# A decoder layer on one Trainium2 core: four sums of the seven-product stage change engine or place, and the routers' due times change

## The chip, the core and the metric

The kernel runs on one core of a Trainium2 chip. The core has five engines that run their own instruction streams and wait for each other by semaphores: TensorE (PE, matmuls), VectorE (DVE), ScalarE (ACT), GpSimd (POOL) and SyncE (SP, which here only issues DMAs). The metric is the device time of one execution in microseconds; the median of the runs counts. A profile of one execution shows what each engine did and when. Times in this document are microseconds from the start of the profiled span unless something else is said.

## The reference

The layer has three residual parts over x, 4 batches of 512 tokens with 512 features, all in float32: attention (32 query heads, 8 key heads, rotary, causal), a product with a context matrix that is rounded in blocks of 128, and a mixture of experts with one shared expert.

```python
x = x + attn(layernorm(x), wq, wk, wv, wo)
x = x + xattn(layernorm(x), ctx_2048)        # both sides rounded to 8 bits in blocks of 128
x = x + moe(layernorm(x), Wg, W1, W3, W2, sw1, sw3, sw2)

def moe(xt, ...):                            # 2048 tokens, 8 experts, 256 places each
    probs = softmax(xt @ Wg); eidx = argmax(probs); gate = probs[eidx]
    pos = place of the token among those of its expert; keep = pos < 256
    oe = (silu(xd @ W1[e]) * (xd @ W3[e])) @ W2[e]      # xd: the tokens sorted by expert
    shared = (silu(xt @ sw1) * (xt @ sw3)) @ sw2
    return oe[place] * gate * keep + shared
```

## The kernel before

**The attention loop.** A loop written out at build time goes over 80 pieces of attention, each of two half steps, n = 0 to 159, 40 half steps (SPB) for a batch. In each half step TensorE does scores (L939), turns the exponentials (L989) and multiplies with v (L1020); VectorE takes minima and ACT exponentials between them. These steps alone would leave TensorE waiting, so other work is put between them.

**The planner.** That other work is a list of jobs (L742 to L818), each a Python generator with a due half step, a cost in ns of TensorE time, a rank (`want`, or the due time where there is none; less 4 for the kinds in CHAIN) and the jobs that must be over before it. `Fill.upto` (L862) issues pieces of jobs in order of rank until its account of TensorE time reaches a goal. `share(n)` (L1066) sets how many ns a half step is to be filled with: it goes through the jobs in order of rank, adds up what is left of each in `ahead`, and for every q, k, v or o job takes `ahead` over the half steps that remain until it is wanted; the largest of these, kept between an even share (3522 to 3842 ns for batches 0 to 2) and 5284, is the quota.

```python
            ahead += job.left * (n < (B - 1) * SPB or job.key[0] not in CHAIN)
            if job.want > n + 20:
                break
            if job.key[0] in "qkvo":
                most = max(most, ahead / max(job.want - n, 1))
```

Some pieces ask for room on VectorE (`yield "dve", lag, us`) and some also for a moment in which GpSimd is idle by the planner's account (`"quiet"`; the helper `gpsimd(us, ...)` at L272 issues a GpSimd operation and adds `us` to that account). All of GpSimd's two-input operations are recorded at that helper's line, L273. A lag is counted in half steps of 7250 ns.

For each batch b the jobs that follow attention are: `o` (the output projection, four of them), `s` (sums of the second layernorm), `c` (the context matrix, rounded), `t` (four groups of 128 tokens: rounding, product with the context, sum into `acc`) and `w`, the **router**. The router (L617) writes the rows of `acc` to x2 in device memory by SP, makes the third layernorm, turns it and writes it to h3d by ACT's queue (L642), computes the logits (L655), counts the places by matmuls (L688, L689) and then scatters the rows to the experts' places xd by four indirect DMAs on GpSimd's queue (L719). It starts when all four `t` of its batch, and `cs` of the next batch, are over.

**After the loop** (from 1085 us) the shared expert is made in units (L1338 on): `shared_up(b, c)` for blocks c of 128 hidden columns, then two `shared_down(b, j)` for each batch. Between the matmuls of a unit, `between` (L1346) issues what is left of batch 3's jobs and of router 2, until nothing is left. A unit counts as one more half step, n = 161 and on. Batch 0 is made by plain matmuls (`up`, L1177). While its blocks run, `weight_sums(c)` (L1246) makes sums of the weights in place on GpSimd.

**The seven products.** For batches 1 to 3 and five of the blocks, `up7` (L1266) computes a 2 by 2 block product with seven products instead of eight. It needs sums of the token blocks, `token_sums(b)` (L1255), t1 to t4, in one buffer xSs for all batches, and the sums of the weights. Each product is four matmuls on 256 columns, gathered in a bank of PSUM: six of them go through the four banks with the tag "sp", product 3 has the single bank with the tag "av". In the version before, product 0 is copied by ACT (p1, L1283), products 1 and 2 are added by VectorE into u2 and u3 (L1284, L1285), product 3 is copied by ACT (p5, L1288) and added to u2 and u3 by two GpSimd sums (in the profile's rows u<-u,p and c<-u,p at L273), products 4, 5 and 6 are added by VectorE (L1291, L1295, L1297), and GpSimd makes the product of the two halves' results (gT<-gT,c).

`token_sums(1)` is called at the end of `shared_down(0, 0)`, `token_sums(b + 1)` at the end of `shared_down(b, 0)` (L1334). `shared_down` adds its two banks into xt on VectorE (L1329).

**The experts** follow (from 1314 us to 1560 us): rows of xd are loaded by SP (L1379), turned on TensorE (`turn_rows`, L257), and each expert's weights are loaded one expert ahead.

Of the kernel before, what the change touches and what calls it, by code (L numbers as in the profile page):

```python
# [23 lines left out]
def decoder_layer(  # L24
# [247 lines left out]
    def gpsimd(us, *args):  # L272
        nc.gpsimd.tensor_tensor(*args)  # L273
        work.gpsimd = max(work.gpsimd, work.at) + 1000 * us
# [469 lines left out]
    def add(due, cost, key, gen, *after, want=None):  # L744

        jobs.append(Job(due, cost, key, gen, after, want))

    MM4 = 4 * 860
    for b in range(B):
        z = b * SPB  # L750
        before = [(("acc", b - 2), 0.7)] if b > 1 else []
        add(z + 5, 0, ("x", b), load(load_x, b), *before)
        if b:
            add(z - 18, 0, ("wv", b), load(load_v, b), (("q", b - 1, 11), 0.5))
            add(z - 24, 0, ("hx", b), load(load_h, b), *([(("zero",), 0.7)] if b == 1 else []))
            add(z - 22, 0, ("hs", b), job_hs(b), (("hx", b), 1))
            add(z - 16, 1760, ("h", b), job_h(b), (("hs", b), 1.5), (("q", b - 1, 4 * NG - 1), 0))
        for j in range(TB):
            if b or j:
                add(  # L760
                    z - 16, MM4, ("v", b, j), job_v(b, j), (("h", b), 0.2), (("wv", b), 1.5),
                    want=z - 4 + 0.8 * j,
                )
        for a in range(NG):
            za = z + 10 * a
            if za:
                if a == 0:
                    before = ("q", b - 1, 4 * NG - 1)
                else:
                    before = ("q", b, 4 * a - 5) if a > 1 else ("v", b, TB - 1)  # L770
                n = b * NG + a
                add(
                    za - 20, 0, ("wk", b, a), load(load_k, b, a),
                    *([(("k", *divmod(n - 2, NG)), 0.5)] if n > 2 else []),
                )
                add(za - 20, 0, ("wq", b, a), load(load_q, b, a), (before, 0.5))
                add(
                    za - 10, MM4, ("k", b, a), job_k(b, a),
                    (("h", b), 0.2), (("wk", b, a), 1.5),
                    want=za - 4.5,  # L780
                )
            for r, due in enumerate((-9.5, -8.5, -7, -5)):

                want = 2 * r - 3.7 if a < NG - 1 or b == B - 1 else 0.8 * r + 1.1
                if za or r > 2:
                    add(
                        za + due, MM4, ("q", b, 4 * a + r), job_q(b, 4 * a + r),
                        (("h", b), 0.2), (("wq", b, a), 1.5), want=za + want,
                    )
            n = b * NG + a  # L790
            before = [(("o", *divmod(n - 1, NG)), 0.7)] if n else []
            if b == B - 1 and a > 1:
                before = [(("o", b, 1), 0.7)] if a == 3 else []
            add(za + 5, 0, ("wo", b, a), load(load_o, b, a), *before)
            add(za + 7, 110, ("r", b, a), job_r(b, a), want=za - 20)
            add(za + 8, 0, ("m", b, a), job_m(b, a), (("r", b, a), 1.5 if n < B * NG - 2 else 1), want=za - 20)
            add(za + 10, 0, ("n", b, a), job_n(b, a), (("m", b, a), 0), want=za - 20)
            add(
                za + 10, 4 * MM4, ("o", b, a), job_o(b, a),
                (("wo", b, a), 1.5), (("x", b), 1), (("n", b, a), 0.6),  # L800
                want=za + ((21, 21, 17, 16.5) if b < B - 1 else (22, 19.5, 18, 16.5))[a],
            )
        before = [(("t", b - 1, j), 0) for j in range(TB)] if b else []
        add(z + 6, 220, ("cs", b), job_cs(b), *([(("w", b - 2), 0.7)] if b > 1 else []))
        add(z + (22 if b else 12), 4 * 220, ("c", b), job_c(b), (("cs", b), 0.2), *before)
        ze = z + SPB + (5 if b < B - 1 else 0)
        add(ze, 0, ("s", b), job_s(b), (("o", b, NG - 1), 1))
        for j in range(TB):
            add(
                ze + 2 + (0, 3, 3, 2)[B - 1 - b] * j, 8 * 220, ("t", b, j), job_t(b, j),  # L810
                (("s", b), 0), (("c", b), 1), *([(("t", b, j - 2), 0)] if j > 1 else []),
            )
        add(ze + 5, 4 * 440 + 4000, ("w", b), job_w(b), *[(("t", b, j), 1) for j in range(TB)], *([(("cs", b + 1), 0)] if b < B - 1 else []))
    add(8, 0, ("zero",), job_zero())
    jobs.sort(key=lambda x: x.rank())
    for key in [("h", 0)]:
# [429 lines left out]
    def weight_sums(c):  # L1246

        a11, a12, a21, a22 = blocks(c)
        s2, s3, s4 = (wS[:, i, :, c * P : (c + 1) * P] for i in range(3))
        gpsimd(0.66, s3, a11, a21, ALU.subtract)  # L1250
        gpsimd(0.66, a21, a21, a22, ALU.add)
        gpsimd(0.66, s2, a21, a11, ALU.subtract)
        gpsimd(0.66, s4, a12, s2, ALU.subtract)

    def token_sums(b):  # L1255

        x = h3x[b]
        b11, b12, b21, b22 = (x[:, k : k + 2, t : t + T2] for k in (0, 2) for t in (0, T2))
        t1, t2, t3, t4 = (xSs[:, i] for i in range(4))
        gpsimd(1.27, t1, b12, b11, ALU.subtract)  # L1260
        gpsimd(1.27, t3, b22, b12, ALU.subtract)
        gpsimd(1.27, t2, b22, t1, ALU.subtract)
        gpsimd(1.27, t4, b21, t2, ALU.subtract)
        xS[b] = t1, t2, t3, t4, b11, b21, b22

    def up7(b, c, mid):  # L1266
        a11, a12, s1, a22 = blocks(c)
        s2, s3, s4 = (wS[:, i, :, c * P : (c + 1) * P] for i in range(3))
        t1, t2, t3, t4, b11, b21, b22 = xS[b]

        def product(i, w, x):
            ps = bank("av" if i == 3 else "sp", f"p7_{b}_{c}_{i}")[:, 0:T2]
            for k in range(2):
                nc.tensor.matmul(ps, w[:, k, :], x[:, k, :], start=k == 0, stop=k == 1)  # L1274
            return ps

        def part(tag, bufs=2):
            return gp.tile([P, T2], F32, tag=tag, bufs=bufs, name=f"{tag}_{b}_{c}")

        g = gTs[b][:, c, :]  # L1280
        p1, p5, u2, u3 = part("p1"), part("p5", 1), part("u2"), part("u3")
        c2 = gp.tile([P, T], F32, tag="c2", bufs=2, name=f"c2_{b}_{c}")
        nc.scalar.copy(p1, product(0, a11, b11))  # L1283
        nc.vector.tensor_tensor(u2, product(1, s2, t2), p1, ALU.add)  # L1284
        nc.vector.tensor_tensor(u3, product(2, s3, t3), u2, ALU.add)  # L1285
        if mid:
            mid(2500, 1.3)
        nc.scalar.copy(p5, product(3, s1, t1))  # L1288
        gpsimd(0.66, u2, u2, p5, ALU.add)
        gpsimd(0.66, c2[:, T2:T], u3, p5, ALU.add)  # L1290
        nc.vector.tensor_tensor(g[:, 0:T2], product(4, a12, b21), p1, ALU.add)  # L1291
        nc.scalar.activation(g[:, 0:T2], g[:, 0:T2], AF.Silu)
        if mid:
            mid(1700)
        nc.vector.tensor_tensor(g[:, T2:T], product(5, s4, b22), u2, ALU.add)  # L1295
        nc.scalar.activation(g[:, T2:T], g[:, T2:T], AF.Silu)
        nc.vector.tensor_tensor(c2[:, 0:T2], product(6, a22, t4), u3, ALU.add)  # L1297
        gpsimd(1.27, g, g, c2, ALU.mult)
        if mid:
            mid(1700, 1.0)  # L1300

    def shared_up(b, c, mid=None):
        if b not in gTs:
            gTs[b] = gp.tile([P, NHC, T], F32, tag="gT", bufs=2, name=f"gT_{b}")
        if b and c < HF:
            up7(b, c, mid)
        else:
            up(se["w"][0], h3x[b], gTs[b], c, T, f"s{b}_{c}", mid)
        if not b and c < HF:
            weight_sums(c)  # L1310
        if c == (HF - 1 if b else HF):
            se["next"] = b + 2
            load_h3(b + 2)
# [10 lines left out]
    def shared_down(b, j, mid=None):  # L1324
        for i in range(b * TB + j, b * TB + j + 2):
            xtile(i)
        for k, py in enumerate(down(gTs[b], se["w"][1], j, f"ys_{b}_{j}", "sp", mid)):
            i = b * TB + j + k
            nc.vector.tensor_tensor(xts[i], py, xts[i], ALU.add)  # L1329
            if i in routed:  # L1330
                nc.sync.dma_start(out=outf[i * P : (i + 1) * P, :], in_=xts[i])
            elif i not in kept:
                nc.sync.dma_start(out=x2[i * P : (i + 1) * P, :], in_=xts[i])
        if j == 0 and b < B - 1:  # L1334
            token_sums(b + 1)

    kept = set()
# [205 lines left out]
```

## Time and profile before

| what | us |
|---|---|
| median of three runs (lowest, highest) | 1594.07 (1592.9, 1597.47) |
| the profiled execution | 1587.93 |
| its span, first to last instruction | 1586.2 |
| TensorE busy | 1545.7 |
| VectorE busy | 849.8 |
| ACT busy | 529.5 |
| POOL busy | 405.1 |

By stage, from the windows view (us; busy time of each engine):

| stage | length | PE | DVE | ACT | POOL |
|---|---|---|---|---|---|
| 1085.4 to 1170.5: batch 0 of the shared expert, rest of the jobs | 85.1 | 84.46 | 49.13 | 14.58 | 40.89 |
| 1170.5 to 1215.6: seven products of batch 1 and half its "down" | 45.1 | 42.40 | 27.51 | 8.84 | 27.96 |
| 1230 to 1266: seven products of batch 2, router 3 | 36.0 | 35.28 | 16.95 | 10.56 | 12.20 |
| 1279.9 to 1316: seven products of batch 3 | 36.1 | 32.97 | 11.37 | 9.44 | 16.31 |
| 1316 to 1586.2: experts and the end | 270.2 | 264.62 | 47.06 | 25.84 | 16.33 |

How to read it: the profile's time line gives the start of an instruction, its length, its engine and line, the operation, what it writes and reads by the program's names, how many were merged into the row, and in brackets how long the engine sat idle before it and what ended that. A group's row has the busy time and mean ns of one after the bar, then the idle time before such instructions. A row of the windows view has the window, its length, and the busy time and number of instructions of PE, PEld (weight loads), DVE, ACT and POOL, the granted TensorE clock, and the DMA share and GB/s. The granted clock is 1.00 in all but two short stretches near 631 and 925 and at the very end.

### The profile page before, as it was taken

The numbers are of one execution on the slowest core, as the hardware profiler recorded it, in microseconds if no ns is written. First come the engines' busy times: TensorE is split into PE (matmuls) and PEld (weight loads), VectorE is DVE, ScalarE is ACT, GpSimd is POOL, SyncE is SP. The second block draws the span as 40 slices with busy tenths as digits, with TensorE's granted clock in tenths as the row PEclk, the third lists the DMA queues.
The fourth block names the chain that finished last, engine by engine and source line by source line (L and its number), as shares of the span: only waits on it lengthen the run. The fifth ranks groups of instructions, "written<-read, shape, count | busy, mean of one in ns | idle before, by whom it ended". The sixth has DMA issues, their size and how long they took to land.

```text
span 1586.2 us, 20493 instructions
## 1 busy us (share of the span) xinstructions
PE 1545.7 (97%) x6839; PEld 888.4 (56%) x6844; DVE 849.8 (54%) x2459; ACT 529.5 (33%) x1586; POOL 405.1 (26%) x370
## 2 busy tenths in 40 slices
PE   9999999999999999999999999999999999999998
PEld 5555555555544554555555545555455867776773
DVE  4465843458756566787656575665665431111114
ACT  2344453434444433443444444552111321110100
POOL 2021310303343031334312133143365340000004
PEclk9999999999999999999999999999999999999999
DMA  4474431524325253432525342256150350654646
GB/s 140 130 229 134 100 101 47 140 92 102 101 61 151 75 133 101 127 91 69 147 80 144 117 100 61 60 159 187 40 186 27 103 190 19 222 196 139 224 148 225
DMA packets 118346, 194.31 MB, mean 123 GB/s; under 512 B 17120, under 2 KB 36576, under 8 KB 117728
## 3 DMA queue, kind: packets, MB, share of 16 engines
q10 hardware_dynamic: 65472, 100.94, 22.7%
q1 hardware_dynamic: 50208, 83.67, 17.3%
q0 software_dynamic: 2560, 8.39, 1.6%
q8 instruction: 54, 0.88, 0.2%
q14 instruction: 52, 0.43, 0.1%
HBM read 135.54 MB, written 28.05 MB: 103 GB/s over the span
## 4 chain that ended last, share of the span: by engine, by line
PE 84%; DVE 5%; DMA 5%; POOL 2%; ACT 2%; issue 2%; SPq 1%; ACTq 0%; POOLq 0%; DVEq 0%
PE py L408 13%; PE psq L308 12%; PE p_e L1184 10%; PE sc L939 8%; PE av L1020 8%; PE pt L989 7%; PE p L1274 5%; PE epy L1212 4%; PE psv L350 4%; PE ys L1212 3%; PE psk L308 3%; PE p_s L1184 2%; DMA rrb<-rrd 1%; ACT pm L972 1%; PE ptr_h L257 1%
## 5 line engine op out<-in xcount | busy, mean ns | idle before, releaser
L972 ACT ACTIVATE pm<-pm,mn 128x256 f32<-128x256 f32 (+3 forms) x512 | 281.0, 550 | 381.5 <-DVE mn L962 352.5
L962 DVE CUSTOM_DVE_ANT_0 pm<-sc,mask 128x256 f32<-128x256 f32 (+3 forms) x512 | 216.8, 485 | 83.9 <-PE sc L939 83.6
L408 PE MATMUL py<-wo,aT 128*128 128x512 f32 x512 | 238.1, 599 | 1.5 <-issue 0.9
L308 PE MATMUL psq<-hT,wq 128*128 128x512 f32 x512 | 237.6, 601 | 1.7 <-DVE y L604 1.6
L273 POOL TENSOR_TENSOR t1q<-t1q,tsq 128x512 f32<-128x512 f32 x64 | 82.9, 1296 | 395.4 <-DMA tsq<-t2q 193.9
L939 PE MATMUL sc<-kT,t1q 64*128 64x384 f32 (+3 forms) x1024 | 169.2, 450 | 10.8 <-DVE pT L1006 3.5
L1006 DVE COPY pT<-pt 128x128 f32<-128x128 f32 (+3 forms) x256 | 114.0, 484 | 113.6 <-PE pt L989 106.0
L989 PEld LDWEIGHTS pt<-ident,pm 128*128 128x128 f32 x1280 | 145.0, 142 | 39.7 <-issue 28.7
L989 PE MATMUL pt<-ident,pm 128*128 128x128 f32 x1280 | 156.2, 275 | 4.1 <-DVE mn L962 4.0
L1184 PE MATMUL p_e<-h3x,slot_e 128*128 128x256 f32 x704 | 155.1, 380 | 0.0
L1020 PE MATMUL av<-pT,v 128*64 128x512 f32 (+3 forms) x1024 | 152.3, 439 | 1.2 <-ACT pT L1000 1.2
L308 PEld LDWEIGHTS psq<-hT,wq 128*128 128x128 f32 x512 | 92.3, 191 | 102.2 <-issue 97.7
L1000 ACT COPY pT<-pt 128x128 f32<-128x128 f32 (+3 forms) x256 | 96.9, 431 | 155.6 <-PE pt L989 123.6
L408 PEld LDWEIGHTS py<-wo,aT 128*128 128x128 f32 x512 | 92.1, 190 | 96.3 <-issue 88.6
L1184 PEld LDWEIGHTS p_e<-h3x,slot_e 128*128 128x128 f32 x704 | 132.6, 190 | 22.8 <-issue 5.3
L939 PEld LDWEIGHTS sc<-kT,t1q 64*128 64x128 f32 x1024 | 85.4, 186 | 94.3 <-issue 61.2
L1020 PEld LDWEIGHTS av<-pT,v 128*64 128x64 f32 x1024 | 68.3, 136 | 107.7 <-issue 95.6
L273 POOL TENSOR_TENSOR acc<-acc,y 128x512 f32<-128x512 f32 x64 | 81.0, 1270 | 136.1 <-DVE y L604 104.2
L972 ACT ACTIVATION_READ_ACCUMULATOR pm<-pm,mn 128x1 f32 x512 | 95.6, 187 | 0.0
L273 POOL TENSOR_TENSOR aT<-aT,rrb 128x512 f32<-128x512 f32 x64 | 82.0, 1311 | 18.6 <-DMA rrb<-rrd 9.7
L1196 DVE TENSOR_TENSOR wS<-p_e,wS 128x256 f32<-128x256 f32 x40 | 17.0, 424 | 119.3 <-PE p_e L1184 119.3
L1455 POOL DMA_INDIRECT slot_e<-oe,gidx x16 | 15.9, 996 | 243.7 <-DMA oe<-yo 239.1
(201 smaller groups left out, 1690.2 us busy)
## 6 DMA issues: line engine op xcount, KB each, us to landing
slot_e<-in_L_ffn_W_dram SPq DMA_DIRECT2D x14, 1280.0 KB, 12.3
wq<-in_L_attn_wq_dram ACTq DMA_DIRECT2D x16, 1024.0 KB, 6.4
tsq<-t2q SPq DMA_DIRECT2D x256, 64.0 KB, 2.3
wo<-in_L_attn_wo_dram ACTq DMA_DIRECT2D x16, 1024.0 KB, 5.6
rrb<-rrd ACTq DMA_DIRECT2D x32, 512.0 KB, 7.4
slot_e<-in_L_ffn_W_dram SPq DMA_DIRECT2D x7, 1408.0 KB, 6.7
kT<-t1k ACTq DMA_DIRECT2D x64, 128.0 KB, 2.9
wv<-in_L_attn_wv_dram ACTq DMA_DIRECT2D x4, 1024.0 KB, 6.1
```

The source lines that it names most:

```text
L273: nc.gpsimd.tensor_tensor(*args)
L308: nc.tensor.matmul(ps, w[:, k, c0 : c0 + P], hTs[b][:, k, :], start=(k == 0), stop=(k == KC - 1),)
L408: nc.tensor.matmul(py, aT[:, r, j * P : (j + 1) * P], wts["o", a][:, r, :], start=(r == 0), stop=(r == 3),)
L939: nc.tensor.matmul(scs[g][:, o : o + nk], qTs[b, p][g * HD : (g + 1) * HD, it * P : nk], kTs[b, p // 2][g * HD : (g + 1) * HD, 0:nk], star ...
L962: nc.vector.tensor_tensor_reduce(out=pm[:, o : o + nk], in0=scs[g][:, o : o + nk], in1=mask[:, T - nk : T], scale=-(HD**-0.5), scalar=3.0e ...
L972: nc.scalar.activation(pm[:, o : o + nk], pm[:, o : o + nk], AF.Exp, bias=mn, scale=-1.0, accum_out=rss[b, a][:, col : col + 1],)
L989: nc.tensor.transpose(pt[:, j * P : (j + 1) * P], pms[g][:, j * P : (j + 1) * P], ident)
L1000: nc.scalar.copy(pT[:, 0 : it + 1, it * P : nk], pt[:, o : o + nk].rearrange("p (j t) -> p j t", t=P),)
L1006: nc.vector.tensor_copy(pT[:, it + 1, 0:nk], pt[:, o : o + nk])
L1020: nc.tensor.matmul(av[g * HD : (g + 1) * HD, j * P : T], vs[b][:, j, v0 : v0 + HD], rhs, start=(j == 0), stop=(j == TB - 1),)
L1184: nc.tensor.matmul(pp[:, 0:cols], w13[:, k, o : o + P], xT[:, k, 0:cols], start=(k == 0), stop=(k == KC - 1),)
L1212: nc.tensor.matmul(py, gT[:, c, (t + i) * P : (t + i + 1) * P], w2[:, c, :], start=(c == 0), stop=False,)
```

## The change

There are four edits.

1. The due time of every router, and with it its rank, is later by four half steps.
2. `token_sums`: t3 comes first and stays on GpSimd; for the last batch t1, t2 and t4 are VectorE operations.
3. `up7`: product 3 is no longer copied; VectorE adds its bank into u2 and into the upper half of c2. The tile p5 goes, and the two GpSimd sums and their entries in the planner's account with it.
4. `token_sums(1)` is called in `shared_up(0, 2)`, after the weight sums of block 2, and no longer in `shared_down(0, 0)`.

```diff
-        add(ze + 5, 4 * 440 + 4000, ("w", b), job_w(b), *[(("t", b, j), 1) for j in range(TB)], ...
+        add(ze + 9, 4 * 440 + 4000, ("w", b), job_w(b), *[(("t", b, j), 1) for j in range(TB)], ...
...
-        gpsimd(1.27, t1, b12, b11, ALU.subtract)
         gpsimd(1.27, t3, b22, b12, ALU.subtract)
-        gpsimd(1.27, t2, b22, t1, ALU.subtract)
-        gpsimd(1.27, t4, b21, t2, ALU.subtract)
+        for out, x, y in (t1, b12, b11), (t2, b22, t1), (t4, b21, t2):
+            if b < B - 1:
+                gpsimd(1.27, out, x, y, ALU.subtract)
+            else:
+                nc.vector.tensor_tensor(out, x, y, ALU.subtract)
...
-        nc.scalar.copy(p5, product(3, s1, t1))
-        gpsimd(0.66, u2, u2, p5, ALU.add)
-        gpsimd(0.66, c2[:, T2:T], u3, p5, ALU.add)
+        p5 = product(3, s1, t1)
+        nc.vector.tensor_tensor(u2, p5, u2, ALU.add)
+        nc.vector.tensor_tensor(c2[:, T2:T], p5, u3, ALU.add)
...
         if not b and c < HF:
             weight_sums(c)
+            if c == 2:
+                token_sums(1)
...
-        if j == 0 and b < B - 1:
+        if j == 0 and 0 < b < B - 1:
             token_sums(b + 1)
```

More of the change, by code (lines that the diff above doesn't have):

```diff
@@ L812, in decoder_layer @@
             )
-        add(ze + 5, 4 * 440 + 4000, ("w", b), job_w(b), *[(("t", b, j), 1) for j in range(TB)], *([(("cs", b + 1), 0)] if b < B - 1 else []))
+        add(ze + 9, 4 * 440 + 4000, ("w", b), job_w(b), *[(("t", b, j), 1) for j in range(TB)], *([(("cs", b + 1), 0)] if b < B - 1 else []))
     add(8, 0, ("zero",), job_zero())
@@ L1275, in product, with part @@
             return ps
-        def part(tag, bufs=2):
-            return gp.tile([P, T2], F32, tag=tag, bufs=bufs, name=f"{tag}_{b}_{c}")
+        def part(tag):
+            return gp.tile([P, T2], F32, tag=tag, bufs=2, name=f"{tag}_{b}_{c}")
         g = gTs[b][:, c, :]
-        p1, p5, u2, u3 = part("p1"), part("p5", 1), part("u2"), part("u3")
+        p1, u2, u3 = part("p1"), part("u2"), part("u3")
         c2 = gp.tile([P, T], F32, tag="c2", bufs=2, name=f"c2_{b}_{c}")
```

## The prediction

> **What bounds the kernel.** I read the page first, then TensorE's waits, then the order of time around the longest of them.
>
> ```profile
> PE 1545.7 (97%) x6839; PEld 888.4 (56%) x6844; DVE 849.8 (54%) x2459; ACT 529.5 (33%) x1586; POOL 405.1 (26%) x370
> ...
> PE 84%; DVE 5%; DMA 5%; POOL 2%; ACT 2%; issue 2%; SPq 1%; ACTq 0%; POOLq 0%; DVEq 0%
> ```
>
> TensorE is busy for 1545.7 of 1586.2 us and is 84% of the chain that ended last. No matmul is added or removed, so all that the change can win or lose is TensorE's idle time: 40.5 us. Who ends it (line, waited for: us in total, times, longest):
>
> ```profile
> PE p L1274 <- DVE gT L1295: 3.8, 2, 3.1
> ...
> PE p L1274 <- DVE xt L1329: 2.6, 1, 2.6
> ```
>
> These 6.4 us lie in the seven-product stage that the edits touch; the windows before 1085 us hold some 26 us in about thirty small waits, and 1320 to 1560 us holds none. The 3.1 in order of time, GpSimd (POOL) first:
>
> ```profile
> 1279.33 1.01 POOL L719 DMA_INDIRECT xd<-h,r_dst_i  x1 [4.12 <-DVE r_flat L715]
> 1282.72 0.96 POOL L719 DMA_INDIRECT xd<-h,r_dst_i  x1 [2.38 <-DMA xd<-h,r_dst_i]
> 1285.69 0.96 POOL L719 DMA_INDIRECT xd<-h,r_dst_i  x1 [2.01 <-DMA xd<-h,r_dst_i]
> 1288.68 0.96 POOL L719 DMA_INDIRECT xd<-h,r_dst_i  x1 [2.02 <-DMA xd<-h,r_dst_i]
> 1289.66 0.73 POOL L273 TENSOR_TENSOR u<-u,p 128x256 f32<-128x256 f32 x1
> ```
>
> ```profile
> 1290.42 0.43 DVE L1295 TENSOR_TENSOR gT<-p,u 128x256 f32<-128x256 f32 x1 [5.64 <-POOL u L273]
> ```
>
> ```profile
> 1290.91 1.13 PE L1274 MATMUL p<-xS,wS 128*128 128x256 f32 x4 [3.13 <-DVE gT L1295]
> ```
>
> The last router's four scatters (L719) each wait for the one before to land, 10.3 us from first start to last end. The sum u of the first block of batch 3 stands behind them in POOL's queue, L1295 behind u, and TensorE runs out of the four "sp" banks.
>
> **Sums of p5 on VectorE.** Each of 15 blocks loses an ACT copy and two POOL sums and gains two VectorE sums that read the bank directly. Rows, by form:
>
> ```profile
> L1288 ACT COPY p<-p 128x256 f32<-128x256 f32 x15 | 5.6, 372 | 30.2 <-PE p L1274 30.2
> ```
>
> ```profile
> L273 POOL TENSOR_TENSOR c<-u,p 128x256 f32<-128x256 f32 x15 | 11.4, 763 | 0.0
> ```
>
> ```profile
> L1285 DVE TENSOR_TENSOR u<-p,u 128x256 f32<-128x256 f32 x15 | 6.4, 425 | 4.1 <-PE p L1274 3.6
> ```
>
> L1285 has the same form as the new sums: one input in PSUM, 256 columns. So ACT loses 5.6 us, POOL 11.4 + 10.9 = 22.3, VectorE gains 30 x 0.425 = 12.8. Per block VectorE carries seven such operations, 2.98 us, against seven products at 0.86 us (starts 1279.85, 1280.71 ...), 6.05 us on TensorE. In block (3,0) the product's bank is ready at 1283.58 (where the copy starts now), the sums end at 1284.43, L1291 starts 0.07 later than its 1284.36, and L1295 runs when product 5 is there, at about 1285.3. The 3.13 us go; next late is nothing in this block. POOL's product gT (1.27) still stands behind the scatters until 1291, but its reader is "down", and the first to need its buffer c2 is block (3,2), at about 1295.5. Behind the two new sums, which wait for product 3, VectorE holds L1291, L1295 and L1297, and TensorE's banks wait for those; in the trace product 3 always comes one product ahead of them. The one "av" bank is now held through two sums; it is wanted again 6 us later.
>
> In blocks with fillers a smaller piece: L453 and L241 took 0.83 (twice) and 0.58 us beside a POOL c sum, against 0.43 and 0.17 elsewhere, and TensorE's rows there are 2.29 and 2.08 long instead of 1.89, with a gap of 0.72 at 1243.67. Without the c sums about 0.4 + 0.2 + 0.4 = 1.0 us. Against it: 0.85 us more VectorE work ahead of the fillers; it lies under product 3 to 4. From both sides: 1.7 us gained, 1.5 lost (fillers of 2.8 us plus 0.85 outlast four banks). I take 1.0.
>
> The 2.57 us at 1172.55 I leave standing:
>
> ```profile
> 1169.25 3.31 DVE L251 TENSOR_SCALAR h<-acc,mvb,rsb 128x512 f32<-128x512 f32 x1
> ...
> 1174.38 1.28 DVE L1329 TENSOR_TENSOR xt<-ys,xt 128x512 f32<-128x512 f32 x2
> ```
>
> L251 takes 0.54 in its next row; here it lasted until POOL's acc sums ended at 1172.26, and L1329, which empties the banks, stood behind it. Neither POOL sum nor their order is touched. Bounds: 0 to 2.57 gained.
>
> **Token sums of batch 1**, four POOL sums of 1.27, move from 1152.44-1157.50 to behind block 2's weight sums, which end at 1127.9. POOL is idle 1128.6-1132.7 and 1135-1141; the weight sums of block 3 slip by 5 us and are needed from 1171 on. Their input h3x of batch 1 was asked for at 1085.5. Nothing behind 1157.5 waits for POOL's old place (0.69 us idle before its next sum, for VectorE's y). Cost 0.
>
> **Token sums of batch 3.** Three go to VectorE, behind L1329 (ends 1277.70), before L698. Nearest row: L454, the same form with both inputs in SBUF.
>
> ```profile
> L454 DVE TENSOR_TENSOR qv_x<-qv_x,qm_x x16: 691/692/1634, 378.5 to 1198.5; 128x512 f32<-128x512 f32 x16
> ```
>
> By its median: 3 x 0.69 = 2.08 us, t2 ready at 1279.1, product 1 wants it at 1280.71: hidden. The rule that speaks against the move is in the Trainium skill, "SBUF — State Buffer", Who interferes with whom: a VectorE instruction with two SBUF inputs and a GpSimd instruction reading SBUF exclude each other for the whole instruction. The row's maximum, 1634, shows one such loss of 0.94. If t1 and t2 each met a POOL sum of 1.27, t2 came at 1281.6, 0.9 late. POOL has one such sum then, t3, so I take the row, 0, and keep 0.9. If the router's end follows, it slips by 2.08; the scatters would land at 1293.5 instead of 1291.4, the first expert's rows at 1298.7 instead of 1296.6, wanted at 1307.4: hidden.
>
> **Routers put back.** The due times do not bind: router 0 starts at 506 us, in half step 72 by the count of attention blocks, router 1 in 110, router 2 in 156, router 3 in unit 177, against due 50, 90, 130, 165. All wait for their tokens' last job, so what a router issues (four writes of x2 on SP, four of h3d on ACT, four scatters on POOL, some sixty small VectorE operations) stays where it is in its queues, up to the order among jobs that are ready together. What moves is the rank, by 4: router b (46 + 40b) now comes behind o(b,3) (46.5 + 40b), so share() no longer counts its 5760 ns ahead of o(b,3). Stepping that arithmetic for the old order: half steps 38 to 44 have quotas of 4622, 4536, 4705, 4935, 5267, 5284, 5284 ns; with 5760 less ahead they become 3945, 3858, 4027, 4257, 4589, 5111, 5161, so 3.7 us of matmuls come later; likewise about 4 us in 79 to 84 and 2 us in 115 to 119. TensorE in those stretches and in the ones that follow:
>
> ```profile
> 282.00:327.00 45.00, 45.00 (x189) 22.93 (x188) 19.88 (x62) 17.22 (x57) 11.37 (x10) 1.00 0.47 118
> 327.00:375.00 48.00, 46.70 (x227) 25.10 (x226) 34.17 (x114) 20.13 (x66) 5.25 (x5) 1.00 0.46 131
> ```
>
> The first has no idle time, the second 1.3 us at a quota of 3842. Work moves from a stretch with cover to spare into one without. So 0, but from -4 to +7: every filler after half step 27 shifts a little, and the 26 us of small waits are dealt anew.
>
> **The end of router 3.** Stepping the planner: token sums of batch 1 and p5's sums leave its account of POOL, the quiet steps of t(3,2) and t(3,3) get in one unit earlier, and router 3's last step falls inside down(2,0) instead of after it. Then its scatters stand ahead of t3 in POOL's queue. Its counts matmul would be done near 1268.5 and the first scatter start near 1270.4; plus 10.3 and 1.27 gives t3 at 1282.0, product 2 wants it at 1282.44. Just hidden; each tick of two chunk pairs later costs 1.7 us, at most 5.3 (scatters from about 1276). I take 0.
>
> **Sum.** -3.1 - 1.0 = -4.1 us. The profiled execution took 1587.93 (span 1586.2 and 1.7 around it): 1583.8. It lies 6.1 below the median of the runs, 1594.07; I carry the difference over: 1590.0.
>
> **Rivals.**
> 1. *Quota* (slower). The withheld 10 us leave the attention chain uncovered. It decides above 4.1 us of new idle time. With two thirds lost, +7: 1597. For: the 3842 stretches have idle time. Against: those after them then have more cover. 0.18.
> 2. *t3 behind the scatters.* With 4 us of wait the gain is taken back: 1594. For: my stepping puts them in that order. Against: 0.4 us in hand. 0.15.
> 3. *More goes than I count.* L251 meets no POOL sum (-2.6) and the new deal saves 1.5 us: 1586. For: L251 started 0.53 before POOL's sum at 1169.78, so a small shift parts them. Against: nothing in their order changes. 0.20.
> 4. Forecast, -4.1 with about 2 to each side. 0.47.
>
> What can be told from no change is 0.3%, 4.8 us. Faster than 1589.3: all of 3, two fifths of 4: 0.38. Slower than 1598.9: a third of 1 and the worst of 2, with the tail of both: 0.14. Same: 0.48. The range takes in both ends of the loop's deal less their tails: 1582 to 1598.
>
> **What would show it.** No wait of p on L1295 near the scatters; POOL's u and c rows gone; VectorE sums at 0.42. A wait of p for POOL xS shows rival 2; idle time in half steps 38 to 44, 79 to 84 or 115 to 119 shows rival 1. The forecast is wrong if waits before 1085 us change by over 3 us.

## The result, and the profile after

| | before | after |
|---|---|---|
| median of the timed runs, us | 1595.25 | 1577.3 |
| ratio (95% interval) | | 0.989 (0.9868 to 0.9912) |
| the profiled execution, us | 1587.93 | 1577.95 |
| its span | 1586.2 | 1576.2 |
| TensorE busy, us | 1545.7 | 1543.5 |
| end of the attention loop in it | 1085.4 | 1074.1 |

Faster by 1.1%, below the range of the forecast (1582 to 1598). The page after, its engines and its chain:

```profile
PE 1543.5 (98%) x6844; PEld 887.5 (56%) x6844; DVE 858.7 (54%) x2492; ACT 523.5 (33%) x1571; POOL 380.4 (24%) x337
...
PE 74%; DMA 3%; DVE 3%; POOL 2%; issue 1%; ACT 1%; SPq 0%; ACTq 0%; POOLq 0%; DVEq 0%
```

TensorE's waits after (us in total, times, longest; L1274, L1295 and L1329 of before are now L1277, L1298 and L1334):

```profile
PE p L1277 <- DVE xt L1334: 2.6, 1, 2.6
...
PE p L1277 <- POOL xS L273: 1.4, 1, 1.4
...
PE p L1277 <- DVE gT L1298: 0.3, 1, 0.3
```

The wait of 3.1 us on VectorE's gT is gone as forecast, the 2.6 on xt stays as forecast, and a wait for POOL's xS is new: rival 2, at 1.4 us. All that is far from 18 us. The time is in the attention loop: from its end to the end of the span it is 500.8 us before and 502.1 after; the loop itself is 11.3 us shorter. (The 502.1 hold a stretch at half clock, 1.7 lost, and waits of 2.4 for GpSimd's aT, of which a second profile of the kernel after, e12, has 0.8.) Adding up TensorE's idle time over the loop gives 7.4 us less. A further 1.7 is one stretch at half clock less, and 2.2 more is spread thinly over matmul rows.

The largest single wait in the loop of before is in half steps 86 to 88. VectorE there:

```profile
624.61 0.16 DVE L238 TENSOR_SCALAR veb<-mvb 128x4 f32<-128x4 f32 x1
...
625.87 1.26 DVE L245 TENSOR_TENSOR r0b<-veb,rsb 128x4 f32<-128x4 f32 x1
...
628.14 0.69 DVE L317 TENSOR_TENSOR t2q<-psq,rt 128x512 f32<-128x512 f32 x1
...
629.61 0.45 DVE L251 TENSOR_SCALAR h<-acc,mvb,rsb 128x512 f32<-128x512 f32 x1
630.09 0.69 DVE L460 TENSOR_REDUCE am<-h 128x4 f32<-128x512 f32 x1
630.69 0.28 DVE L962 CUSTOM_DVE_ANT_0 pm<-sc,mask 128x128 f32<-128x128 f32 x1
```

and TensorE, before:

```profile
621.99 1.91 PE L989 MATMUL pt<-ident,pm 128*128 128x128 f32 x16
623.83 2.10 PE L939 MATMUL sc<-kT,t1q 64*128 64x128 f32 x12
625.86 2.37 PE L1020 MATMUL av<-pT,v 128*64 128x512 f32 x16
631.51 3.37 PE L989 MATMUL pt<-ident,pm 128*128 128x128 f32 x16 [3.27 <-DVE mn L962]
```

From 624.6 to 630.7 VectorE works off the root of batch 1's second layernorm (L238 on), three steps of attention itself (L317 among them) and the first token group (L251, L460). The minima (L962) that TensorE's transposes need stand behind them. One step of the root, L245, takes 1.26 where its neighbours take 0.16: it ends with a GpSimd sum that starts in the same moment, so 1.1 of the 3.27 us are that meeting.

```profile
625.86 1.26 POOL L273 TENSOR_TENSOR t1q<-t1q,tsq 128x512 f32<-128x512 f32 x1 [6.90 <-DVE rsb L247]
```

TensorE has nothing else to do: between transposes, scores and av stands no projection, which is the filler here (work of the planner's jobs). Its next transposes take 3.37 instead of 1.9, because half of the clock is withheld from 631.0 on. The same place after:

```profile
620.68 1.91 PE L989 MATMUL pt<-ident,pm 128*128 128x128 f32 x16
622.43 1.02 PE L308 MATMUL psq<-hT,wq 128*128 128x512 f32 x2
623.38 2.00 PE L939 MATMUL sc<-kT,t1q 64*128 64x128 f32 x12
625.31 2.37 PE L1020 MATMUL av<-pT,v 128*64 128x512 f32 x16
627.61 1.97 PE L989 MATMUL pt<-ident,pm 128*128 128x128 f32 x16
```

No wait stands between these rows. By the planner's account the root's step is now issued in half step 89 instead of 87, behind these minima.

**A second figure for each run.** Each run lists the mean granted clock of TensorE. Over 95 runs of the kernel before it lies between 0.988 and 0.998, and the time falls by 1.5 us for each 0.001 that it is higher; time times clock is 1584.1 with a scatter of only 1.3 from run to run. I call this product the time at full clock: a stretch at half clock counts half in it. It separates waits from clock. The kernel after has 1571.6 (8 runs), so 12.5 us of the gain are waits and matmul time, and the rest of about 4 is the clock, 0.9933 to 0.9958. With four to twenty runs a figure at full clock is good to some 0.3 to 0.8 us, no better.

### The profile page after: what moved, and what is told of

The parts are those of the page before. It is cut to its first block, busy times and chain, and to the rows that moved or that the text cites. A ratio compares the mean times of both kernels' runs of the same rounds, so it can differ in the third digit from the quotient of the medians.

```text
span 1576.2 us, 20462 instructions
## 1 busy us (share of the span) xinstructions
PE 1543.5 (98%) x6844; PEld 887.5 (56%) x6844; DVE 858.7 (54%) x2492; ACT 523.5 (33%) x1571; POOL 380.4 (24%) x337
## 4 chain that ended last, share of the span: by engine, by line
PE 74%; DMA 3%; DVE 3%; POOL 2%; issue 1%; ACT 1%; SPq 0%; ACTq 0%; POOLq 0%; DVEq 0%
PE py L408 12%; PE p_e L1184 10%; PE psq L308 9%; PE av L1020 7%; PE sc L939 7%; PE pt L989 6%; PE p L1277 6%; PE epy L1212 4%; PE psv L350 3%; PE p_s L1184 2%; PE ys L1212 2%; PE psk L308 2%; DMA tsq<-t2q 1%; POOL aT L273 1%; PE ptr_h L257 1%
## 5 line engine op out<-in xcount | busy, mean ns | idle before, releaser
L962 DVE CUSTOM_DVE_ANT_0 pm<-sc,mask 128x256 f32<-128x256 f32 (+3 forms) x512 | 216.6, 486 | 91.1 <-PE sc L939 91.1
L308 PE MATMUL psq<-hT,wq 128*128 128x512 f32 x512 | 236.5, 599 | 2.4 <-DVE y L604 2.3
L939 PE MATMUL sc<-kT,t1q 64*128 64x384 f32 (+3 forms) x1024 | 165.5, 448 | 6.7 <-ACT pT L1000 2.5
L308 PEld LDWEIGHTS psq<-hT,wq 128*128 128x128 f32 x512 | 91.9, 190 | 102.1 <-issue 96.4
```

The source lines that it names most:

```text
L308: nc.tensor.matmul(ps, w[:, k, c0 : c0 + P], hTs[b][:, k, :], start=(k == 0), stop=(k == KC - 1),)
L939: nc.tensor.matmul(scs[g][:, o : o + nk], qTs[b, p][g * HD : (g + 1) * HD, it * P : nk], kTs[b, p // 2][g * HD : (g + 1) * HD, 0:nk], star ...
L962: nc.vector.tensor_tensor_reduce(out=pm[:, o : o + nk], in0=scs[g][:, o : o + nk], in1=mask[:, T - nk : T], scale=-(HD**-0.5), scalar=3.0e ...
```

## The experiments

Two groups of theories. For the whole: is it edit 1 (quota) or edits 2 to 4 (sums)? For the quota: "smoothing" (the gain follows the work that is withheld) or "deal" (it comes from where a few VectorE pieces fall).

| run | what | median, us | ratio to before (95%) | at full clock |
|---|---|---|---|---|
| e1_due_only | edit 1 alone | 1581.25 | 0.9915 (0.9898 to 0.9932) | 1573.2 |
| e2_no_due | edits 2 to 4 alone | 1589.14 | 0.9967 (0.9953 to 0.998) | 1582.0 |
| e3_share_only | only share() sees it | 1581.3 | 0.9913 (0.9895 to 0.9931) | 1573.6 |
| e4_before_again | the kernel before | 1594.02 | 0.9996 (0.9982 to 1.001) | 1584.2 |
| e5_three_quarters | routers count 3/4 | 1590.9 | 0.9979 (0.9961 to 0.9997) | 1581.0 |
| e6_share_batch1 | share(), router 1 | 1588.9 | 0.9956 (0.994 to 0.9972) | 1580.7 |
| e7_share_batch2 | share(), router 2 | 1588.7 | 0.9966 (0.9955 to 0.9977) | 1580.6 |
| e9_p5_only | edit 3 alone | 1598.34 | 1.0018 (1.0007 to 1.0028) | 1585.3 |
| e10_t3_vector | after, t3 on VectorE | 1574.83 | 0.9878 (0.9857 to 0.9899) | 1571.0 |
| e11_three_waits | after, three moves | 1575.23 | 0.9875 (0.9842 to 0.9908) | 1569.9 |
| e12_after_again | the kernel after | 1578.83 | 0.9898 (0.9877 to 0.992) | 1571.9 |
| e13_two_waits | after, two moves | 1571.4 | 0.9856 (0.983 to 0.9883) | 1569.2 |

**Which edit.** e1 has the first diff in the kernel before, e2 its reverse in the kernel after; e4 is the kernel before.

```diff
-        add(ze + 5, 4 * 440 + 4000, ...
+        add(ze + 9, 4 * 440 + 4000, ...
```

> The kernel before with the routers' due time alone later by four half steps (edit 1); POOL sums, token sums and their places as before. Its order of work up to the end of the attention loop is that of the changed kernel. Theory A (the gain lies in the attention loop, where the smaller quotas deal TensorE's small waits anew): the loop ends about 11 us earlier than before (1074 instead of 1085 us), the stage after it is as before with its wait of 3.1 us on L1295, and the profiled span is about 1575 us; timed 16 to 18 us below before. Theory B (the gain comes from the POOL sums taken off in the seven products): span within 2 us of 1586, timed within 3 us of before.

> The changed kernel with the routers' due time put back to that of before (edits 2 to 4 alone). Its order up to the end of the loop is that of before. Theory A: the loop ends at 1085 us as before, and the stage after it is 1 to 2 us longer (the wait of 3.1 us on L1295 is gone, waits on POOL for aT and for t3 come): span 1586 to 1588 us, timed within 3 us of before. Theory B: span about 1577 us, timed 15 us or more below before.

> The kernel before, unchanged, for the spans and granted clocks of its timed runs. The profiled execution of before took 1587.93 us, its timed runs 1592.9 to 1597.5, while the changed kernel's profiled and timed runs agree. If short stretches of half clock after waits of 2.5 to 3.3 us come in some executions and not in others, the slower runs have the lower mean clock (each stretch of 3.4 us at half clock costs 1.7 us): 1595 us would go with a clock of about 0.993 against 0.997. If the clock is the same, the 7 us are idle time that comes from something else.

Edit 1 alone brings 10.9 us at full clock, edits 2 to 4 alone 2.1; together they would be 13.0, and 12.5 was measured. The gain of edit 1 was put to zero in the prediction. The sizes expected here were off as well: the median of e1 fell by 12.6 and not by 16 to 18, and e2 came out 4.8 below before and not within 3.

**Rank or quota.** e3 leaves every rank as it was and lets `share` alone count the routers later:

```diff
+        def later(x):
+            return x.rank() + 4 * (x.key[0] == "w")
-        for job in sorted(todo, key=lambda x: x.rank()):
+        for job in sorted(todo, key=later):
...
-            if job.want > n + 20:
+            if later(job) > n + 20:
```

> The kernel before, where only share() counts the routers four half steps later; due times and ranks of the jobs themselves stay. Theory A1 (quota): as e1, span about 1575 us. Theory A2 (the rank among jobs that are ready together): as before, span 1586 us.

1573.6 at full clock against 1573.2 in e1: the quota explains all of it within the noise.

**What in the quota.** e5 counts the routers at 3/4 in their old place. e6 and e7 let share() move one router only, otherwise as in e3 (e7 has 2 for the 1):

```diff
-            ahead += job.left * (...)
+            ahead += job.left * (0.75 if job.key[0] == "w" else 1) * (...)
...
+            return x.rank() + 4 * (x.key == ("w", 1))
```

> The kernel before; share() counts the routers at three quarters of their cost, in their old place. By the planner's account this brings its loop near the put-back one's at two places: the second layernorm's last step for batch 1 leaves half step 87 for 89, and the last group of tokens of batch 0 leaves half step 71 for 69; but it takes little off the quotas (half step 43: 5283 to 4394, half step 78: 5283 to 4438, half steps 79 to 84 unchanged or higher). Theory 'smoothing' (time falls with the work withheld): a quarter of the count, so about a quarter of the 12.6 us of the share-only kernel, near 1590.5. Theory 'deal' (what counts is between which minima and transposes a few pieces with VectorE work fall): most of the gain, the idle time of 3.3 us near 628 and those of 1.4 to 1.6 near 419, 447 and 484 gone, loop end near 1076 instead of 1085.4, median near 1583.

> The kernel before; share() counts the router of batch 1 alone four half steps later. Quotas fall in half steps 79 to 84 only (5141 to 4373, 5096 to 4168), about 4 of the 10 us withheld; the last output projection of batch 1 ends in half step 85 instead of 84, but the second layernorm's root and the first token group's piece still stand in half steps 87 and 88. Theory 'smoothing': four tenths of 12.6, near 1589. Theory 'deal': the 3.3 us near 628 stay, the median within 2 us of 1593.9.

> The kernel before; share() counts the router of batch 2 alone four half steps later. Quotas fall in half steps 115 to 119 (5283... of before is 4464 to 3880 there), order unchanged before 114. Theory 'smoothing': two tenths of 12.6, near 1591.4. Theory 'deal': the wait of 2.51 near 921 becomes 1.4 and its half-clock stretch of 3.41 us (1.7 lost) goes: 1.1 + 1.7 to 4, near 1590.5; nothing before half step 114 moves. The two theories are told apart here only by the place: idle time must change near 921 and nowhere else.

"Deal" missed twice. In e5 the pieces moved as it said, but only 3.1 us at full clock were gained: the waits near 419, 447 and 484 went and that at 628 fell to 1.19, but waits of 2.41 at 351.6, 2.67 at 587.0 and 2.40 at 861.1 came. In e6 the wait at 628 went although the root stayed ahead of the minima (only L251 and L460 moved behind them, to 629.61). TensorE and VectorE in e6:

```profile
619.70 1.91 PE L989 MATMUL pt<-ident,pm 128*128 128x128 f32 x16
621.45 4.46 PE L308 MATMUL psq<-hT,wq 128*128 128x512 f32 x10
625.84 2.00 PE L939 MATMUL sc<-kT,t1q 64*128 64x128 f32 x12
627.76 2.37 PE L1020 MATMUL av<-pT,v 128*64 128x512 f32 x16
```

```profile
626.91 0.16 DVE L247 SCALAR_TENSOR_TENSOR rsb<-r0b,rsb 128x4 f32<-128x4 f32 x1
627.01 0.29 DVE L962 CUSTOM_DVE_ANT_0 pm<-sc,mask 128x128 f32<-128x128 f32 x1
```

Ten projection matmuls (L308) stand where before has none: the lower quota of half steps 79 to 84 left them over, and they cover the root. "Smoothing" has the number of e5 (1590.5) and e6 (1589), but not of e7: the wait near 921 fell from 2.51 to 1.38, waits of 0.59 near 867 and 0.47 near 936 went, nothing before half step 114 moved, and yet 3.5 us at full clock were gained, as much as in e6. Its shares, four and two tenths, came from the prediction's 10 us. The quotas that share() gives when the kernels are built fall by 23.7 us in all for e3, by 18.6 for e5, 5.4 for e6 and 2.1 for e7, against gains of 10.5, 3.1, 3.4 and 3.5: the gain does not follow the work withheld.

So neither theory stands as stated; what the traces show is a number of single waits. The one at 628 needs two things at once, a VectorE piece ahead of what TensorE waits for (e8 below takes it away) and no filler to cover it (e6 supplies it). The old quota made the second: by the planner's account all filler that was ready was spent by half step 87, and 87 and 88 had none. At 484 it looks the same: before has no projection between 478 and 491, after has fourteen there, of which twelve are

```profile
485.62 5.31 PE L350 MATMUL psv<-wv,hT 128*128 128x512 f32 x12
```

At 447 and 921 projections stand right beside the wait, so the pair of conditions is shown for 628 alone. By e6 and e7 routers 1 and 2 bring 3.4 and 3.5; the first would have 3.6 by difference from e3, but was not run alone, and e6 removes the wait at 628 in another way (by filler) than the kernel after (the root later).

e8 moves the root, and with it the token group that follows it. A second hunk of its edit acts after the loop, so only its loop can be compared (one execution, 1598.42):

```diff
-        yield "quiet", 0.3, 2.0
+        yield "quiet", 2.0 if b == 1 else 0.3, 2.0
```

> The kernel before; of batch 1 the root of the second layernorm (some sixteen small VectorE operations, 3.5 us) is held for two half steps instead of 0.3, so that it falls into half step 89 and no longer ahead of half step 88's minima; and token sums that come before their rows first finish that batch's router, so the part after the loop is not comparable and only the loop is read. Theory 'deal': the idle time of 3.27 us near 628 (pt waits for mn) is gone, under 0.5, with quotas up to there as before; half step 88 ends 3 us earlier, 5 if the half-clock stretch goes with it. Theory 'smoothing': the idle time stays, since the quotas up to there are those of before.

```profile
626.18 2.37 PE L1020 MATMUL av<-pT,v 128*64 128x512 f32 x16
628.49 1.97 PE L989 MATMUL pt<-ident,pm 128*128 128x128 f32 x16
```

The transposes follow av at once, with the quota of before up to there: this wait has the named cause. (Later in the loop e8 met waits of 1.4 to 1.6 at 696, 724 and 762, like those that before has one batch earlier, at 419, 447 and 484: a gain at one place moves the next.)

**Edit 3 alone,** in the kernel before (one line of it):

```diff
-        gpsimd(0.66, u2, u2, p5, ALU.add)
+        nc.vector.tensor_tensor(u2, p5, u2, ALU.add)
```

> The kernel before with edit 3 alone (product 3 added by VectorE from its bank, no copy, no GpSimd sums). Theory 'as forecast' (each edit's cost stands alone): the 3.13 us on L1295 go and nothing comes: about 3 to 4 us below the kernel before, near 1591. Theory 'edits belong together': router 3's end comes one step earlier by the planner's account, its four scatters stand ahead of the last batch's token sums, which here are all on GpSimd in the order t1, t3, t2, t4; t2 comes 2.5 us after the place at which edits 2 to 4 together have t3 (1.37 us of wait for product 2), and product 1 wants it 0.86 earlier: 1.37 + 2.54 + 0.86 = 4.8 us of wait for POOL xS. Then the sum is -3.1 - 1 + 4.8 = +0.7, near 1595.5.

```profile
PE p L1274 <- POOL xS L273: 4.7, 1, 4.7
```

The wait is as worked out (4.8): the sums on VectorE alone make the kernel slower, by 1.2 us at full clock where 0.7 was worked out, since router 3's scatters then stand ahead of all four token sums. The rest of the median's 1598.3 is clock (0.9922 on average). Edits 2 and 4 together pay for edit 3; they were not run apart. In the kernel after, POOL and TensorE at that place:

```profile
1263.03 1.01 POOL L719 DMA_INDIRECT xd<-h,r_dst_i  x1 [1.37 <-DVE r_flat L715]
1266.05 0.96 POOL L719 DMA_INDIRECT xd<-h,r_dst_i  x1 [2.01 <-DMA xd<-h,r_dst_i]
1269.02 0.96 POOL L719 DMA_INDIRECT xd<-h,r_dst_i  x1 [2.01 <-DMA xd<-h,r_dst_i]
1272.60 0.96 POOL L719 DMA_INDIRECT xd<-h,r_dst_i  x1 [2.62 <-DMA xd<-h,r_dst_i]
1273.59 1.27 POOL L273 TENSOR_TENSOR xS<-h3x 128x512 f32<-128x512 f32 x1
```

```profile
1274.91 1.13 PE L1277 MATMUL p<-xS,wS 128*128 128x256 f32 x4 [1.36 <-POOL xS L273]
```

**Taking more waits away.** e10 adds t3 to the three sums on VectorE. e13 adds the second edit below, e11 all three; e12 is the kernel after.

```diff
-        gpsimd(1.27, t3, b22, b12, ALU.subtract)
-        for out, x, y in (t1, b12, b11), (t2, b22, t1), (t4, b21, t2):
+        for out, x, y in (t1, b12, b11), (t2, b22, t1), (t3, b22, b12), (t4, b21, t2):
...
-        yield "dve", 0, 1.3
+        yield "quiet" if b == B - 1 and j > 1 else "dve", 0, 1.3
...
-        yield "dve", 0.8 * pace(b), 1.6
+        yield "dve", 0.4 if b == 0 else 0.8 * pace(b), 1.6
```

> The changed kernel with t3 of the last batch on VectorE as well. The wait of 1.36 us of product 2 for POOL's xS behind the four scatters goes; VectorE has 0.69 more ahead of the scatters' indices, hidden. Theory 'rival 2 is what held the tail back': -1.4 of the changed kernel's time, near 1575.9, TensorE waits for nothing between 1265 and 1280 by more than 0.3. Other theory: another reason (banks, VectorE) is late right behind it, and the time stays at 1577.

> The changed kernel with three waits of TensorE above 1.3 us aimed at: t3 of the last batch on VectorE (1.36); the first pieces of the last two token groups of batch 3 only when GpSimd is idle by the planner's account (the 2.57 at 1163, L251 held by GpSimd's sums ahead of L1334); router 0's last VectorE operations with a lag of 0.4 instead of 0.8 half steps (the 2.43 at 584, where nine of its operations of 0.16 took 1.1 to 1.2 us each beside GpSimd's four aT products). If all three go: 6.4 us, and the half-clock stretches that followed two of them in the changed kernel's profile, 1.7 each in part of the runs: 1577.3 - 6.4 - 2 = near 1569. If the moved pieces meet another GpSimd operation instead, the waits come back at other places and the time stays within 3 us of the run with t3 alone.

> The changed kernel once more, for more runs beside the others: 1577.3 within 2 us. Its idle time by half step should repeat within 0.3 us of the first profile's at every wait above 1 us; half-clock stretches of 3.41 us, if there are any, should follow waits of TensorE above about 1.2 us and not fall at the same places in each profile.

> The changed kernel with two of the three moves of the run before: t3 of the last batch on VectorE, and the first pieces of the last two token groups of batch 3 only when GpSimd is idle by the planner's account; router 0's end as in the changed kernel. If the 2.57 us at 1163 are a VectorE operation held by GpSimd's sums ahead of L1334, they go here as well: idle time 1.36 + 2.57 = 3.9 less than the changed kernel, and the half-clock stretch behind 1163 with them. From the 1574.8 of t3 alone: -2.6 and up to 1 for the clock, near 1571.5; the wait of 2.4 to 2.8 near 585 stays. If the other move was what took the wait at 1163 away (by its shift of the loop), the wait comes back and the time is 1574.8.

e10: the 1.36 us are gone, and nothing over 0.3 came behind them. At full clock that is 0.6, with an uncertainty as large; the rest of its 2.5 to 4 us in the median is clock. e12: its median is within the 2 us, but the wait near 585 was 2.80 there against 2.43, more than the 0.3 allowed, and two of its half-clock stretches stand at the same waits as in the first profile of after. e13: the wait at 1163 is gone, 1571.4 where 1571.5 was expected. The row that had held it, L251, took 3.31 ahead of the banks' L1334 in the kernel after; in e13 it takes 0.54 behind them (L1333 and L1276 of e13 are L1334 and L1277 of after):

```profile
1156.91 1.29 DVE L1333 TENSOR_TENSOR xt<-ys,xt 128x512 f32<-128x512 f32 x2 [1.31 <-PE ys L1222]
...
1160.04 0.54 DVE L251 TENSOR_SCALAR h<-acc,mvb,rsb 128x512 f32<-128x512 f32 x1
```

TensorE then runs without a gap there:

```profile
1156.81 1.13 PE L1276 MATMUL p<-h3x,slot_s 128*128 128x256 f32 x4
1157.77 1.89 PE L1276 MATMUL p<-xS,wS 128*128 128x256 f32 x8
```

e13 is the best version: 1.4% below the kernel before (1.2 to 1.7), and some 6 us below the one after. e11 missed: its third move should have freed the wait of 2.4 to 2.8 near 585. In the kernel after, VectorE there:

```profile
579.86 1.11 DVE L704 TENSOR_TENSOR r_flat<-r_flat,r_cnt 128x4 f32<-128x4 f32 x1
581.01 1.19 DVE L708 TENSOR_TENSOR r_dst<-r_flat,spill 128x4 f32<-128x4 f32 x1
...
583.45 1.19 DVE L710 TENSOR_TENSOR r_dst<-r_dst,spill 128x4 f32<-128x4 f32 x1
...
585.42 0.69 DVE L317 TENSOR_TENSOR t2q<-psq,rt 128x512 f32<-128x512 f32 x1
```

```profile
579.69 4.93 POOL L273 TENSOR_TENSOR aT<-aT,rrb 128x512 f32<-128x512 f32 x4
```

```profile
586.81 2.83 PE L408 MATMUL py<-wo,aT 128*128 128x512 f32 x3 [2.43 <-issue]
```

Router 0's small operations take 0.16 each elsewhere. Beside the four GpSimd products, from 579.69 to 584.62, L704 to L710 take about as long as one product each, and L317, the first to read a bank, stands behind them all. (The profile names no engine for TensorE's 2.43; that it is a bank is inferred from L319, behind L317, which ends at 586.71.) Moving the small operations freed them, and a larger operation met the same products. VectorE, GpSimd and TensorE in e11:

```profile
581.52 7.04 DVE L456 TENSOR_TENSOR qq_c<-qv_c,qm_c 128x512 bf16<-128x512 f32 x1
```

```profile
581.88 4.91 POOL L273 TENSOR_TENSOR aT<-aT,rrb 128x512 f32<-128x512 f32 x4
586.76 1.25 POOL L273 TENSOR_TENSOR t1k<-t1k,tsk 128x512 f32<-128x512 f32 x1
```

```profile
588.62 0.40 PE L257 MATMUL ptr_c<-ident_b,qq_c 128*128 128x128 bf16 x4 [3.68 <-DVE qq_c L456]
```

The wait there grew to 3.68. An order that frees both wasn't tried.

## Why the prediction was wrong, and where it was right

By its steps:

- **Sums of p5 on VectorE, -3.1:** right. The wait is gone, and the new sums take what L1285 took, by the group's row after. (The scatters came earlier too, so no run tells whether the sums alone would have been enough.)

```profile
L1292 DVE TENSOR_TENSOR u<-p,u 128x256 f32<-128x256 f32 x15 | 6.4, 424 | 7.1 <-PE p L1277 7.1
```

- **Fillers, -1.0:** right. The gap of 0.72 at 1243.67 is 0.32 after, and the rows of 2.29 and 2.08 are 1.89. From the first of the seven products to the last there are 143.9 us in before and 141.4 in e2: 2.5 less, where -3.1, -1.0 and the 1.4 for t3 (below) make 2.7.
- **The 2.57 on L1329 left standing:** right, 2.57 after. e13 shows its cause to be the one read off then, GpSimd's acc sums holding L251.
- **Token sums of batch 1, 0:** right, no wait comes between 1100 and 1160.
- **Token sums of batch 3, 0 or 0.9 by the Trainium skill's rule of the exclusive port ("SBUF — State Buffer", Who interferes with whom):** the row decided rightly: 0.68 for t1, 1.42 for t2 and t4 together. The rule was not put to the test there, since GpSimd ran only a scatter meanwhile; it has weight elsewhere (L245 in the kernel before, L704 to L710 in the one after, L456 in e11).
- **The end of router 3, "Just hidden":** the order was right, the size wrong. I had the first scatter 12.0 us ahead of product 2's want; it came 10.5 ahead, so t3 was 1.36 late and not 0.44 early. Rival 2's mechanism, a third of its price.
- **"Routers put back ... So 0, from -4 to +7": this step failed.** The loop gained 10.5 to 10.9 us at full clock (e3, e1). Two things were wrong in it. First, the stepping: the old quotas are right, the new ones are not. For half steps 38 to 44 share() of the changed kernel gives 4040, 4007, 3979, 4037, 4005, 3964 and 3911 ns, where 3945 rising to 5161 was worked out, and it falls in 70 to 78 as well (5284 to between 4676 and 3842), which the prediction does not have. By the planner's account work comes up to 4.3 us later in half steps 44 and 45, where 3.7 was said, but up to 10.3 us *earlier* in 69 to 78: the kernel before had next to nothing to issue in 68 and 69. Second, the test: I looked where work would be missing (stretches at 3842 with idle time) and not where it would arrive. Half steps 87 and 88 had no filler at all under the old quota, because it had all been spent; the 3.27 us at 628 stood in the waits as the largest of the loop, with its cause, and were counted among "small waits" to be dealt anew. The prediction's own sign came: waits before 1085 us changed by 7.4, more than 3.
- **Rivals 1 and 3:** rival 1 has the sign wrong for the same reason. Rival 3 had the right sign: of its two parts L251 brought nothing, and the new deal was put at 1.5 us, a seventh of what it brought.
- **Carrying over the 6.1 us between the profile and the median:** failed as well, and with it "all that the change can win or lose is TensorE's idle time". That distance is the clock: the profiled run of before had 0.997, its runs 0.9933 on average. A change that takes long waits away takes part of it along; after, profile and median differ by 0.7.

Against the forecast of -4.1: at full clock -12.5, of which edits 2 to 4 have 2.1 and the loop the rest, and some -4 by the clock.

Near 921 the profile names "issue" as the end of the wait, but it shows more. In before TensorE goes on at 923.97, 0.12 us after the first minimum (L962) has read its bank; in e7 the same distance is 0.11. Ahead of that minimum stand a root and a token group once more. How router 2's quota moves them by a microsecond was not worked out, and that is open. Open too are the 2.2 us spread over matmul rows, and what edits 2 and 4 do one by one.

## What to carry to other kernels

When work is spread by a planner, look for the stretches in which it has nothing left to issue, and at which VectorE piece stands ahead of TensorE's next operand there; a lower rate earlier can be the gain, as it was at 628. Of two edits that belong together, price each without the other: one alone may be slower. And before a profile's distance to the median is carried over, compare the granted clocks.

## What the runs showed of the hardware

**A wait of TensorE can cost half a window of clock.** In the fifteen profiles the half-clock stretches (the one at the very end apart) are 3.41, 6.83 or 10.24 us long, and within a profile they start on one grid of 3.413 us. I laid that grid over the 14 profiles that have such a stretch and took the windows that were at full clock themselves. Of those in which TensorE was idle for 2.02 us or more, 30 of 30 were followed by half clock; of those with 1 to 2.02 idle 7 of 90, of the others 1 of some 6,250. (The border of 2.02 was read off these same windows, and many of them hold the same few waits.) The grid lies elsewhere in each execution. So a wait of 2 to 3 us, which may fall across a border of the grid, brought a stretch in 20 of 32 cases over all fifteen profiles, one of 3 and more in 11 of 16, one of 1 to 2 in 7 of 93. Each 3.41 us at half clock are 1.7 us lost. The 2.57 on xt had its stretch in the profile of after (at 1167.2) and none in that of before. The Trainium skill ("TensorE: Matmul & The Clock Gate", Part 1) has the free-running window of 3.41 us, but speaks of an idle window, and under "Why this matters for your kernels" of gaps over about 3; here some 2.0 us of idle time within one window were enough.

**One VectorE operation waited out five GpSimd operations.** L456 (two inputs in SBUF, 0.69 us elsewhere) lasted 7.04 us in e11, beside five GpSimd operations without a pause between them. The Trainium skill ("SBUF — State Buffer", Who interferes with whom) has whoever issues first hold the shared ports for its whole instruction. It does not say when the one that waits gets its turn: here L456 got none until GpSimd's queue paused, while L704 to L710 in the kernel after, and L454 in the kernel before (1.63 at 858.65), got theirs behind one GpSimd operation. What makes the difference is not shown.
